# A transformer block on one core: the last addition moved to ScalarE and a DMA, another split of the convolution, and a new order

## The chip, the cores and the metric

The kernel runs on one core of a Trainium2 chip. A core has five engines that work side by side, each through its own list of instructions in order: TensorE (PE, matrix products; its weight loads are listed as PEld), VectorE (DVE), ScalarE (ACT), GpSimd (POOL) and SyncE (SP, which only issues transfers). Sixteen DMA engines move data; they are fed by the queues of SP, ACT and POOL. The metric is the device time of one execution in microseconds (us); less is better.

## The reference

The input x has 16 images of 128 channels and 96 x 96 pixels, all float32. One block is computed, image by image:

```
x_hwc = x.transpose(0, 2, 3, 1)
xn1 = _layernorm(x_hwc, ln1_w, ln1_b)
attn_out = _attention(xn1, wq, wk, wv, wp)     # 8 heads; channels attend to channels, over all pixels
x = x + attn_out.transpose(0, 3, 1, 2)
xn2 = _layernorm(x_hwc, ln2_w, ln2_b)          # x_hwc of the new x
h1 = einsum('bchw,oc->bohw', xn2, w_in)        # 128 -> 512 channels
h2 = depthwise 3x3 convolution of h1, padded by 1
h3 = gelu(h2, approximate=False)
x = x + einsum('bchw,oc->bohw', h3, w_out)     # 512 -> 128 channels
```

The attention needs one 128 x 128 matrix per image (the Gram matrix of the normalised pixels), so the whole image must have passed the first layer norm (LN1) before its attention is known. The second part needs only neighbouring rows.

## The kernel before, in words

**Tiling.** An image is cut in 8 bands of 12 rows (1152 pixels), a band in 3 units of 4 rows (384 pixels); 16 images make 128 bands. Channels lie on the 128 partitions. The 512 hidden channels are 4 chunks of 128.

**LN1 and LN2** take groups of four times 128 pixels: PE transposes them into PSUM (`forth`, L602), DVE takes statistics (`stats`, L609), POOL makes the variance and the power -0.5 of it (`variance` L616, `power` L620), for LN2 DVE makes a shift (`shift`, tile `nb_b`, L624), ACT scales into a buffer `zT` (L647, L651; for the start DVE takes half of it, L634, L638), PE adds to the Gram matrix (L661, LN1 only) and transposes back (L692), and ACT places the result in the padded image `xn` (L696, L698). While one image is in its second part, LN1 of the next runs beside it.

**x2.** PE applies the attention's matrix (L560). ACT writes the sum with a bias to the band buffer `xb` (`mixed`, L569), and a DMA issued by POOL adds x to it in flight (`add_x`, L572). There are 6 `xb` buffers. The first 6 bands of image 0 have x in `xb` already, and DVE adds (L566).

**Hidden part.** For a chunk of a band (`conv_job`), PE makes the hidden rows (L877), ACT copies them to SBUF (`kept`, L882; two rows from the band above by `halo`, L873). The depthwise convolution has 9 taps. One comes with the first DVE instruction; of the 8 others, two, or three for chunk 1, are products by ACT (`products`, L890, tiles `pr`, 5 buffers) that POOL-issued DMAs add to each other and to the result (L899); the rest are DVE instructions (`tap`, L895: one scalar_tensor_tensor over 128 x 1152 each). ACT applies gelu (L903). The very last job has no products.

**Chunk 3 on PE.** In some bands (`by_pe`) chunk 3 is not convolved so: 9 matmuls per unit with a composed 128 x 128 matrix per tap (`by_matmuls`, L945) make the convolved hidden rows in PSUM directly, and ACT applies gelu from there (L951). Before, these are every second band, and 6 of the last 8.

**Out.** Four matmuls per unit (`ffn_out`, L968) sum the chunks in PSUM, DVE adds that to `xb` (L975), SP stores the band (L979).

**Order.** Nothing runs in the order of the loops. Each operation is recorded with an estimated duration and a place, a number that its kind's entry in the table `AT` shifts; `Plan.order` then runs a list scheduling with those numbers, buffers included, and the instructions are emitted in the order of the planned starts. Operations with a smaller place go first when several are ready. At run time each engine follows its list and waits on semaphores, so an instruction that waits holds up all behind it on its engine. POOL's list holds both the small arithmetic of the layer norms and the issues of the accumulating DMAs.

Of the kernel before, what the change touches and what calls it, by code (L numbers as in the profile page):

```python
# [17 lines left out]
UR = 4  # L18
BR = 12
PE_CHUNK = 3  # L20
PE_BANDS = (0,)
PE_OF = 2
# [4 lines left out]
THIRD, THIRD_OF, THIRD_CHUNK = (0, 1, 2), 3, 1  # L27
# [3 lines left out]
X1_BUFS, XB_BUFS, PR_BUFS, H3_BUFS, ZT_BUFS = 2, 6, 5, 10, 3  # L31
IN_TURN = ("tr", "h3", "pr", "xb", "x1")
AT = dict(
    weights=86, zeros=34, load_a=-17.95, forth_a=-1.35, stats_a=-23.85, variance_a=50.15, power_a=-16.45,
    scaled_a=6.1, gram=-31.8, back_a=-145.85, place_a=68, attention=-19.55, mix=-17.6, residual=60.15,
    mixed=-98.2, add_x=-22.85, forth_b=-2, stats_b=-5.55, variance_b=52.05, power_b=-11, shift_b=-76.95,
    scaled_b=98.5, back_b=-23.15, place_b=20.55, halo=21.65, hidden=1.35, kept=-79.55, products=8.4,
    add_last=-64.4, tap=0.1, add_first=-14.5, gelu=-63.5, conv=1.15, conv_gelu=-1.85, out=4.9, add=-43.45,
    store=47.1,
# [6 lines left out]
T_WEIGHTS = 20000  # L46
# [160 lines left out]
def tile_restormer_block(  # L207
# [133 lines left out]
    grams, mats, h3s, staged = {}, {}, {}, {}  # L341
# [5 lines left out]
    def at(kind, place):  # L347
        return place + AT[kind]
# [56 lines left out]
    def weights(p):  # L405
# [17 lines left out]
        def transposed(parts, kept, gives):  # L423

            key = ("weights", next(names))
            h = ("h", key)
            d = {}

            def forth():
                d["pt"] = bank(key)  # L430
                for k, part in enumerate(parts()):
                    nc.tensor.transpose(d["pt"][:, k * P : (k + 1) * P], part, ident)

            pe(440, at("weights", p), forth, mine, [h])
            dve(700, at("weights", p), lambda: kept(d["pt"]), [h], [("w", g) for g in gives] + mine[1:])
# [56 lines left out]
        def unit_parts():  # L492
# [3 lines left out]
        op("ACT", 400, at("load_a", p), loads, [], mine, T_WEIGHTS, dma=2 * T_MOVE)  # L496
# [3 lines left out]
            lambda: [v["wqk"][:, :P], v["wqk"][:, P:], v["wp"], wv_sb], keep_qkp, ["qk"]  # L500
# [6 lines left out]
        dve(700, at("weights", p), unit_parts, [mine[0], ("w", "in")], [mine[1]])  # L507
        transposed(
            lambda: [v["wt"][:, n, :] for n in range(NCH)],
            lambda pt: nc.vector.tensor_scalar(winT.rearrange("p n c -> p (n c)"), pt, w2, None, ALU.mult), ["in"],  # L510
        )
        transposed(
            lambda: [v["wout"][:, n * P : (n + 1) * P] for n in range(NCH)],
            lambda pt: nc.vector.tensor_copy(woutT.rearrange("p n c -> p (n c)"), pt), ["out"],
        )
        for t0 in (0, 4, 8):
            ts = range(t0, min(t0 + 4, 9))
            dve(170 * len(ts), at("weights", p), lambda ts=ts: comp_parts(ts), [mine[0]], [mine[1]])
            transposed(
                lambda ts=ts: [v["wt"][:, t % 4, :] for t in ts],  # L520
# [23 lines left out]
    def norm(i, second, place_of):  # L544
# [8 lines left out]
        def x2(s, u):  # L553
# [22 lines left out]
            if loaded:  # L576
                pe(t_mm(UT), at("mix", s), mix, [*ins, xtok(u)], [pm])
                dve(t_dve(UT), at("residual", s), residual, [pm], [xtok(u)])
                return
            pe(t_mm(UT), at("mix", s), mix, ins, [pm, xtok(u)])  # L580
            act(t_act(UT, 1) - 43, at("mixed", s), mixed, [pm], [xtok(u)])
            if u % UPB == UPB - 1:
                xb = [xtok(b * UPB + k) for k in range(UPB)]
                add(at("add_x", s), add_x, [], xb)

        def pixels(s, m):
# [5 lines left out]
            by_dve = QT // 2 if early else 0  # L592

# [32 lines left out]
            def zT(q):  # L626
                zTs[q] = zT_bufs[plan.slot["zT", (name, q)]]
                return zTs[q]
# [38 lines left out]
            for q, tr in zip(qs, trs):  # L667
                units = {t // TPU: None for t in range(q * QT, (q + 1) * QT)}
                pe(110 * QT, at("forth" + ab, s), lambda q=q: forth(q), [xtok(u) for u in units], [tr])
            for j in range(QB * QT // 2):  # L670
                dve(341, at("stats" + ab, s), lambda j=j: stats(j), [trs[2 * j // QT]], [bt])
            op("POOL", T_VARIANCE, at("variance" + ab, s), variance, [], [bt], T_VARIANCE + 33 + SLACK)
            op("POOL", T_POWER, at("power" + ab, s), power, [], [bt], T_POWER + 33 + SLACK)
            if second:
                dve(80, at("shift" + ab, s), shift, [], [bt])
            for h, (q, tr) in enumerate(zip(qs, trs)):
                zt, sh = ("zT", (name, q)), s + STEP["scaled"] * h
                if by_dve:
                    dve(by_dve * 240, at("scaled" + ab, sh), lambda q=q: also_scaled(q), [tr, bt], [(*zt, 0)])
                act((QT - by_dve) * (343 if second else 250), at("scaled" + ab, sh), lambda q=q: scaled(q), [tr, bt], [(*zt, 1)])  # L680
                if not second:
                    pe(QT * 220, at("gram", sh), lambda q=q: gram(q), [(*zt, 0), (*zt, 1), ("w", "ones")], [("g", i)])

        def channels(s, u):
# [27 lines left out]
            pe(110 * TPU, at("back" + ab, s), back, [("zT", (name, q), k) for q in quads for k in range(2)], [pb])  # L712
            act(t_act(UT, 1) - 43 if second else t_copy(UT), at("place" + ab, s), place, [pb, ("w", "shift")], [z_unit(i, u)])
            for k, r, row, of in copies:
                act(225, at("place" + ab, s), lambda k=k, r=r, row=row: place_row(k, r, row), [pb, ("w", "shift")], [("z", k, of)])
# [243 lines left out]
    def ffn_out(p, g, s):  # L959
# [13 lines left out]
        def add():  # L973
            xt = x_unit(xbs, i, s + b * UPB)
            nc.vector.tensor_add(xt, d["po"], xt)  # L975

# [7 lines left out]
        dve(t_dve(UT), at("add", p), add, [po], [("xb", (i, b), s)])  # L984
        if g == NG - 1:
            move(at("store", p), lambda: store(s, 1), [("xb", (i, b), s)], [], T_MOVE / UPB)
        elif s == UPB - 1:
            move(at("store", p), lambda: store(0, UPB), [("xb", (i, b), k) for k in range(UPB)], [], T_MOVE)
# [64 lines left out]
```

## Time and profile before

| what | value |
|---|---|
| median of 3 executions | 4179.18 us (4177.25 to 4179.65) |
| the profiled execution | 4194.94 us, its span 4193.2 us |
| PE busy | 4151.7 us, 99% |
| DVE busy | 4073.2 us, 97% |
| ACT busy | 3682.0 us, 88% |
| POOL busy | 2593.8 us, 62% |
| DMA traffic | 827.63 MB, mean 197 GB/s; HBM 53 GB/s |
| mean granted TensorE clock | 0.998 |

The profile is of one execution, and its rows are compared with its own span; the execution with the profiler was 15.8 us longer than the median without. A group of instructions is given as: line, engine, operation, out<-in, count, then busy time, mean duration in ns, and idle time of the engine just before them with what ended it. A float32 matmul over 128 x 384 appears as two records. Busy time of PE is modelled at its ends, and the duration of a DVE or ACT instruction overlaps the start of the next, so the price of one more instruction is better read from the distance of starts in a row of equal instructions.

### The profile page before, as it was taken

What the parts mean: (1) busy time and instruction counts of PE and PEld (TensorE: products, weight loads), DVE (VectorE), ACT (ScalarE), POOL (GpSimd) and SP (SyncE); (2) the same over time, 40 slices, a digit from 0 to 9 for tenths busy, and PEclk for the clock granted to TensorE, in tenths of its full rate; (3) what the DMA queues carried; (4) which work ended last, traced back from release to release, by engine and by line L of the source; (5) the groups of instructions that cost most, each with busy time, mean ns of one, the idle gap of its engine ahead of it and who ended that gap; (6) DMA issues with size and microseconds to landing.
All of it is one profiled execution on the core that took longest, in us unless ns stands there. A gap on an engine that the chain in (4) does not pass through costs nothing. (4 is left out here: it accounts for less than half of the span.)

```text
span 4193.2 us, 52283 instructions
## 1 busy us (share of the span) xinstructions
PE 4151.7 (99%) x17457; PEld 2684.0 (64%) x17457; DVE 4073.2 (97%) x4676; ACT 3682.0 (88%) x6970; POOL 2593.8 (62%) x2373
## 2 busy tenths in 40 slices
PE   8999999999999999999999999999999999999999
PEld 6666666666666666666666666666666666666565
DVE  6999999999999999999999999999999999999998
ACT  4988989899899888999988899898998989889885
POOL 3656666566675666657666566656656667565542
PEclk9999999999999999999999999999999999999999
DMA  2999999999999999999999999999999999999997
GB/s 78 192 191 201 208 198 208 189 213 201 206 207 204 206 196 204 203 202 207 198 206 198 197 206 198 206 201 201 208 197 212 195 207 202 191 205 199 196 197 160
DMA packets 203934, 827.63 MB, mean 197 GB/s; under 512 B 23568, under 2 KB 24976, under 8 KB 203664
## 3 DMA queue, kind: packets, MB, share of 16 engines
q0 software_dynamic: 164160, 672.47, 82.9%
q1 hardware_dynamic: 37152, 151.01, 9.8%
q8 instruction: 138, 2.26, 0.2%
q10 hardware_dynamic: 2352, 0.81, 0.1%
q14 instruction: 132, 1.08, 0.1%
HBM read 148.26 MB, written 75.50 MB: 53 GB/s over the span
## 5 line engine op out<-in xcount | busy, mean ns | idle before, releaser
L895 DVE SCALAR_TENSOR_TENSOR h<-h,ratio,h 128x1152 f32<-128x1152 f32 x2104 | 2933.0, 1415 | 5.0
L890 ACT ACTIVATE pr<-h,ratio 128x1152 f32<-128x1152 f32 x1018 | 1304.2, 1290 | 21.8 <-DMA pr<-pr 20.3
L945 PE MATMUL h<-xn,comp 128*128 128x384 f32 x3564 | 1277.4, 486 | 1.7 <-ACT h L951 0.9
L968 PE MATMUL h<-h,woutT 128*128 128x384 f32 x3072 | 1112.8, 487 | 1.8 <-ACT h L903 0.7
L877 PE MATMUL h<-xn,winT 128*128 128x384 f32 (+1 forms) x2676 | 1048.4, 500 | 2.1 <-DVE x L975 1.1
L945 PEld LDWEIGHTS h<-xn,comp 128*128 128x128 f32 x3564 | 647.3, 189 | 394.4 <-issue 10.4
L899 POOL DMA_DIRECT2D pr<-pr x573 | 545.7, 960 | 475.1 <-ACT pr L890 325.7
L968 PEld LDWEIGHTS h<-h,woutT 128*128 128x128 f32 x3072 | 560.7, 190 | 345.1 <-issue 7.5
L882 ACT COPY h<-h 128x384 f32<-128x384 f32 (+1 forms) x1338 | 658.1, 521 | 139.7 <-PE h L877 122.4
L877 PEld LDWEIGHTS h<-xn,winT 128*128 128x128 f32 x2676 | 479.5, 190 | 290.9 <-issue 49.7
L899 POOL DMA_DIRECT2D h<-pr x445 | 433.9, 977 | 356.7 <-DVE h L895 93.7
L895 DVE SCALAR_TENSOR_TENSOR h<-h,ratio 128x1152 f32<-128x1152 f32 x446 | 630.1, 1419 | 11.5 <-ACT h L882 7.8
L903 ACT ACTIVATE h<-h 128x1152 f32<-128x1152 f32 x448 | 533.7, 1192 | 51.9 <-DMA h<-pr 48.0
L616 POOL TENSOR_SCALAR ve_b<-st_b 128x4 f32<-128x4 f32 x288 | 364.3, 1265 | 310.8 <-DVE st_b L609 304.6
L620 POOL TENSOR_TENSOR rstd_b<-ve_b,mhalf 128x4 f32<-128x4 f32 x288 | 525.1, 1823 | 13.9
L620 POOL TENSOR_TENSOR rstd_a<-ve_a,mhalf 128x4 f32<-128x4 f32 x288 | 498.2, 1730 | 15.7 <-POOL ve_a L616 0.2
L616 POOL TENSOR_SCALAR ve_a<-st_a 128x4 f32<-128x4 f32 x288 | 323.9, 1125 | 292.2 <-DVE st_a L609 291.7
L651 ACT ACTIVATE zT<-pT_b,nb_b,rstd_b 128x128 f32<-128x128 f32 x1132 | 431.4, 483 | 45.7 <-DVE nb_b L624 45.4
L647 ACT ACTIVATE zT<-pT_a,rstd_a 128x128 f32<-128x128 f32 x1080 | 314.7, 398 | 39.3 <-POOL rstd_a L620 38.4
L661 PEld LDWEIGHTS g<-zT 128*128 128x128 f32 x2304 | 294.4, 192 | 50.0 <-ACT zT L647 7.9
L661 PE MATMUL g<-zT 128*128 128x129 f32 x2304 | 307.1, 276 | 3.3 <-ACT zT L647 3.3
L560 PE MATMUL h<-xn,mwT 128*128 128x384 f32 x768 | 283.5, 490 | 1.2 <-ACT x L569 0.8
(172 smaller groups left out, 3605.4 us busy)
## 6 DMA issues: line engine op xcount, KB each, us to landing
pr<-pr POOLq DMA_DIRECT2D x573, 576.0 KB, 6.9
h<-pr POOLq DMA_DIRECT2D x445, 576.0 KB, 7.4
x<-in_x_dram SPq DMA_DIRECT2D x128, 576.0 KB, 6.5
out_dram<-x SPq DMA_DIRECT2D x127, 576.0 KB, 5.6
x<-in_x_dram POOLq DMA_DIRECT2D x122, 576.0 KB, 7.7
out_dram<-x SPq DMA_DIRECT2D x3, 192.0 KB, 1.9
weights<-in_L_conv_w_in_dram ACTq DMA_DIRECT2D x1, 256.0 KB, 10.7
weights<-in_L_conv_w_out_dram ACTq DMA_DIRECT2D x1, 256.0 KB, 11.6
```

The lines of the kernel that those rows point to most:

```text
L616: nc.gpsimd.tensor_scalar(ve, d["mv"][:, :, 2], 1.0 / C, EPS, ALU.mult, ALU.add)
L620: nc.gpsimd.tensor_tensor(rstd, d["ve"], mhalf, ALU.pow)
L651: nc.scalar.activation(zT(q)[:, k, :P], d["pT", q][:, k, :], AF.Identity, bias=d["nb"][:, t : t + 1], scale=d["rstd"][:, t : t + 1],)
L661: nc.tensor.matmul(grams[i][:, : P + 1], lhsT=zt[:, :P], rhs=zt, start=(q == 0 and k == 0), stop=(q == NU * TPU // QT - 1 and k == QT - 1),)
L877: nc.tensor.matmul(rows(ph), lhsT=winT[:, n, :], rhs=window(xn, r0 + r, e - r, 1), start=True, stop=True)
L882: nc.scalar.copy(window(h1_, r, e - r, 1), rows(d.pop(("ph", r))))
L890: nc.scalar.activation(to, shifted(t), AF.Copy, scale=ratio[:, n, t : t + 1])
L895: nc.vector.scalar_tensor_tensor(h3, shifted(t), ratio[:, n, t : t + 1], onto, ALU.mult, ALU.add)
L899: nc.gpsimd.dma_start(out=to, in_=d["pr", t], accum_op=ALU.add)
L903: nc.scalar.activation(h3, h3, AF.Gelu)
L945: nc.tensor.matmul(d["pc"], lhsT=comp[:, t, :], rhs=window(xn, r0 + dy, UR, dx), start=(t == 0), stop=(t == 8),)
L968: nc.tensor.matmul(rows(d["po"]), lhsT=woutT[:, n, :], rhs=h3s[g, n][:, s * UR : (s + 1) * UR, :], start=(k == 0), stop=(k == NCH - 1),)
```

## The change

Four things:

1. **Final addition.** For all bands but the last two, DVE no longer adds PSUM to `xb`. ACT copies each of the band's three units from PSUM into a buffer of the `pr` pool (`evicted`), and after the third one DMA issued by POOL adds the buffer to `xb` (`add_out`); then SP stores as before.
2. **No third product.** `THIRD` is empty, so chunk 1 has two products like the others, and one more tap on DVE.
3. **Chunk 3 on PE** in bands 0, 2, 4, ... 12 of every 15 (counted from the end) in place of every second; the last 8 bands as before.
4. **Start and order.** LN1 of image 0 scales into buffers of the `h3` pool, a pair of groups in each (9 of 10 buffers hold all 18 groups), in place of 3 `zT` buffers in turn. The weights are loaded by their own place, and the part of their preparation that only the hidden part needs has a place of its own (`late`). All entries of `AT` are new, and image 0 has entries of its own (`..._0`).

```diff
-PE_BANDS = (0,)
-PE_OF = 2
+PE_BANDS = (0, 2, 4, 6, 8, 10, 12)
+PE_OF = 15
-THIRD, THIRD_OF, THIRD_CHUNK = (0, 1, 2), 3, 1
+THIRD, THIRD_OF, THIRD_CHUNK = (), 3, 1
+ADD_OF, ADD_BY_DMA = 1, (0,)
-AT = dict(weights=86, zeros=34, ... stats_b=-5.55, variance_b=52.05, power_b=-11, shift_b=-76.95, ...)
+AT = dict(load_w=10.25, weights=-46.8, ... stats_b=-219.5, variance_b=53.7, power_b=-244.15, shift_b=-78.6, ...)
...
             def zT(q):
-                zTs[q] = zT_bufs[plan.slot["zT", (name, q)]]
+                if q in zTs:
+                    return zTs[q]
+                if not apart:
+                    zTs[q] = zT_bufs[plan.slot["zT", (name, q)]]
+                    return zTs[q]
+                two = [k for k in (q - q % 2, q - q % 2 + 1)]
+                t = h3p.tile([P, BR * W], F32, tag="h3", name=f"zT_{two[0]}")
+                for k in two:
+                    zTs[k] = t[:, k % 2 * QT * (P + 1) : (k % 2 + 1) * QT * (P + 1)].rearrange("p (t c) -> p t c", c=P + 1)
+                    nc.gpsimd.memset(zTs[k][:, :, P:], 1.0)
                 return zTs[q]
...
-        def add():
+        def add_here():
             xt = x_unit(xbs, i, s + b * UPB)
             nc.vector.tensor_add(xt, d["po"], xt)
+
+        def evicted():
+            if s == 0:
+                outs[g] = prp.tile([P, BR, W], F32, tag="pr", name=f"out_{g}")
+            nc.scalar.copy(outs[g][:, s * UR : (s + 1) * UR, :], rows(d["po"]))
+
+        def add_out():
+            nc.gpsimd.dma_start(out=xbs[i, b], in_=outs[g].rearrange("p r w -> p (r w)"), accum_op=ALU.add)
...
-        dve(t_dve(UT), at("add", p), add, [po], [("xb", (i, b), s)])
+        band_ = [("xb", (i, b), k) for k in range(UPB)]
+        if g < NG - 2 and g % ADD_OF in ADD_BY_DMA:
+            act(t_copy(UT), at("evicted", p), evicted, [po], [("pr", ("out", g), s)])
+            if s == UPB - 1:
+                add(at("add_out", p), add_out, [("pr", ("out", g), k) for k in range(UPB)], band_)
+        else:
+            dve(t_dve(UT), at("add", p), add_here, [po], [("xb", (i, b), s)])
```

## The prediction

> **What bounds the kernel now.** I read the busy times first, then the same by stage, then the chain of waits at the end, then what DVE waited for.
>
> ```profile
> PE 4151.7 (99%) x17457; PEld 2684.0 (64%) x17457; DVE 4073.2 (97%) x4676; ACT 3682.0 (88%) x6970; POOL 2593.8 (62%) x2373
> ```
>
> PE and DVE are both nearly full, so the question is how much true work each has. A stage table (busy time, number of instructions, granted clock, DMA share):
>
> ```profile
> core 0: us, PE busy (x) PEld busy (x) DVE busy (x) ACT busy (x) POOL busy (x), PEclk, DMA share, GB/s
> 0.00:104.00 104.00, 87.63 (x541) 71.28 (x542) 65.84 (x195) 49.42 (x129) 39.75 (x97) 0.95 0.25 77
> 104.00:4140.00 4036.00, 4014.39 (x16764) 2583.96 (x16763) 3966.23 (x4448) 3613.30 (x6815) 2547.22 (x2269) 1.00 0.95 201
> 4140.00:4193.00 53.00, 49.64 (x154) 28.77 (x152) 41.11 (x36) 19.33 (x28) 6.88 (x8) 1.00 0.63 147
> ```
>
> DVE idles 104 - 65.84 = 38.2 us in the start, 4036 - 3966.23 = 69.8 us in the long middle, and 53 - 41.11 = 11.9 us at the end: 119.8 us in all. That is all that any change can win on DVE without taking work from it.
>
> ```profile
> L895 DVE SCALAR_TENSOR_TENSOR h<-h,ratio,h 128x1152 f32<-128x1152 f32 x2104 | 2933.0, 1415 | 5.0
> ...
> L945 PE MATMUL h<-xn,comp 128*128 128x384 f32 x3564 | 1277.4, 486 | 1.7 <-ACT h L951 0.9
> L968 PE MATMUL h<-h,woutT 128*128 128x384 f32 x3072 | 1112.8, 487 | 1.8 <-ACT h L903 0.7
> ...
> L975 DVE TENSOR_TENSOR x<-h,x 128x384 f32<-128x384 f32 x384 | 214.2, 558 | 8.8 <-PE h L968 6.8
> ```
>
> ```profile
> 3920.34 5.81 PE h L945 x18
> 4174.16 15.49 PE h L968 x48
> ```
>
> The chain of waits of the last 500 us is matmul after matmul; its two lines give the pace of PE, 5.81/18 = 0.323 us per record of 384 columns. At that pace, with 0.404 for 480 columns and 0.11 for the small ones, PE's work is 1151 (L945) + 992 (L968) + 722 + 178 (L877) + 248 (L560) + 257 (L661) + 502 (4608 transposes) + some 50 = 4100 us of a 4193 us span. DVE's is 4073. So PE is the tighter, by 27 us, and neither has much room.
>
> **The change part by part.** Durations are of the profiled execution; its span stands 14.0 us above the median of 4179.18, and I carry differences over.
>
> *PE.* Bands with chunk 3 on PE: 3564/54 = 66 before; 56 + 6 = 62 after. Removed 4 x 54 records x 0.323 = 69.8 us; added, hidden rows of 4 chunks without halo, 4 x (4 x 0.404 + 2 x 0.323) = 9.0 us. PE: 4100 to 4039.
>
> *DVE.* Removed 378 of the 384 adds: successive starts (an add, then a tap) lie 0.467 us apart, 176.5 us. Added: taps go from 445 x 6 - 128 + 8 = 2550 to 449 x 6 + 8 = 2702; starts in a row of taps lie 1.328 us apart, so 152 x 1.328 = 201.9 us. DVE: +25.4, to 4098.6 us. So the two engines change places: work on the fuller engine falls by 1 us only, and what counts is how much of DVE's idle time goes once PE has 61 us of slack.
>
> *ACT.* 378 copies at 0.37 between starts (140 us) and 4 jobs' copies, products and gelus (18) come; 128 products at 1.157 (148) and 12 small gelus (5) go: +5 us, on an engine that idles 420 us in the middle. A copy waits for its matmuls as the add did on DVE (6.8 us in 16 waits); behind it on ACT stand the copies of hidden rows and the products, and behind those wait DVE's taps (7.8 us now) and POOL's issues; the PSUM bank (one of 4) is held as long. Taken as hidden, since ACT is the less full engine.
>
> *DMA.*
>
> ```profile
> q0 software_dynamic: 164160, 672.47, 82.9%
> q1 hardware_dynamic: 37152, 151.01, 9.8%
> ```
>
> The 1140 accumulating transfers take 0.829 x 4193 / 1140 = 3.05 us each of all sixteen engines. After: 449 + 449 + 126 + 122 = 1146. 6 more: 18 us, and six more issues of about 0.96 us on POOL. The engines are at 0.95 in the middle, so 5% (about 200 us) covers it; without cover it costs 18 us, and with longer queues could cost more. `add_out` stands in POOL's list behind the third copy on ACT, as `add_x` stands behind its copies; that wait costs POOL 79.4 us in 122 issues, so some 82 us, with variance and power queued behind it, for which the shift on DVE waits; the 128 third additions that go waited 325.7/573 = 0.57 us each, 73 us. No net change. SP's stores now wait for a landing, median 6.9 us, rather than for DVE; SP waits over 1100 us for adds anyway, and `xb` comes free some 8 us later in a cycle of 6 bands (196 us). Zero, bounded by 8 us once for each time the pool runs dry.
>
> *`pr` buffers.* A band's sum stays in one of 5 for two steps between units and a landing, about 20 us; the third product that goes held one for about 10. Taken as zero; bounded above by a stalled product per band, seen in rows as 20.3 us in all today.
>
> *Start.* Before the first hidden matmul at 92.0 us PE has 62.6 us of work, and starts at 5.6: 24 us are gaps or slow clock. In the built order of the changed kernel PE has 3 us more work before that point (LN1 of image 1 is further on), DVE 1 us more before its first tap. The weights move behind the first four groups on ACT's list: five issues of about 0.45 us there, with landings of about 12 us, 15 us before use; 18 more memsets of about 0.1 us stand in front on POOL, done before x lands at 5.6. LN1 of image 0 already keeps PE full at 1.66 us per group, so bigger buffers can only close the gaps around it: between no gain and 8 us; DVE's idle there 30 to 42, I take 32, nearest to closing one third of PE's gaps.
>
> *End.* DVE's 11.9 us are mostly waits for PE (3.4 for one tap, 3.3 for adds); with PE ahead I take 7, between 6 and 14.
>
> *Middle.* DVE's waits:
>
> ```profile
> DVE nb_b L624 <- POOL rstd_b L620: 38.3, 35, 2.0
> DVE x L975 <- PE h L968: 6.8, 16, 2.9
> DVE st_b L609 <- PE pT_b L602: 6.1, 15, 0.9
> DVE x L566 <- PE h L560: 5.9, 6, 2.4
> ```
>
> About 16 of the 69.8 us are waits that PE ended directly; with PE slack they go (0 to 16 remain). 15.6 us are short gaps and the attention chain; they stay. The rest, 38 us, is the wait of the shift for POOL's power, `w`. It does not come from PE:
>
> ```profile
> 1106.77 5.06 POOL L616 TENSOR_SCALAR ve_b<-st_b 128x4 f32<-128x4 f32 x1
> 1105.03 2.75 DVE L895 SCALAR_TENSOR_TENSOR h<-h,ratio 128x1152 f32<-128x1152 f32 x2
> 1107.69 4.08 DVE L895 SCALAR_TENSOR_TENSOR h<-h,ratio,h 128x1152 f32<-128x1152 f32 x3
> 1112.97 0.16 DVE L624 SCALAR_TENSOR_TENSOR nb_b<-st_b,rstd_b 128x4 f32<-128x4 f32 x1 [1.20 <-POOL rstd_b L620]
> ```
>
> A 0.2 us operation on POOL took 5.06 us, ending when a row of five taps on DVE ended, and the shift behind them waited 1.20. POOL gets in only between taps, and not each time. In the built order, one or more POOL instructions stand between variance and power in 142 of 288 groups (121 before; two or more in 4, before 28), and two or fewer taps between statistics and shift in 9 groups (20 before). By this trace's waits sorted by the first count (0.078 us without one, 0.243 with one), w would be 45; by the second 36; by the sum now 38. Below these: LN2's statistics and power move to the front of their queues (`stats_b`, `power_b`), so POOL gets the work sooner. I take 30, in 20 to 62; the top is 0.215 us for every group, near what a group with one issue between pays.
>
> [...]
>
> *Sum.* 4098.6 + 32 + 7 + (0 + 30 + 15.6) = 4183.2, 10.0 below 4193.2: 4169 us as the median.
>
> **Rivals.**
>
> *Nothing moves (same).* The change does not do what it says, since DVE stays as full as PE was: w keeps 38, the start 38.2. 4098.6 + 38.2 + 7 + 53.6 = 4197.4, so about 4183; with half of those gains 4176. For it: work on the fuller engine falls by 1 us. Against: PE's gaps in the start look closable.
>
> *POOL's power is late (slower).* Place: the shift in DVE's list, every LN2 group. Price w = 62: span 4215, median 4201. It decides from w = 48: then the span passes 4201.6, which is 0.2% above. For it: 152 more taps, 378 fewer adds. Against: two or fewer taps in front of the shift become rarer.
>
> *DMA engines become the pace (slower).* At 0.95 in the middle, 3909 us of work grow by 18 us; if time follows, 4193 x 18/3909 = 19.6 us: 4199. For it: the middle's share. Against: DVE names DMA in no wait of the middle.
>
> *A better start still and few waits (faster).* Start 30, end 6, w 20: 4098.6 + 30 + 6 + 35.6 = 4170: 4156. Slightly below, about 4148, lies what is left if half of the short gaps go as well.
>
> *TensorE slows when it has gaps.*
>
> ```profile
> 144.42 0.33 PE L692 MATMUL pB_b<-ident,zT 128*128 128x128 f32 x1 [2.18 <-ACT zT L651]
> 147.03 5.08 PE L968 MATMUL h<-h,woutT 128*128 128x384 f32 x8 [0.46 <-ACT h L882]
> ```
>
> After waits of 2.18 and 0.72 us and shorter ones, 8 records took 5.08 us in place of 2.6, with 0.72 of the clock granted from 141 to 153 us. In the middle it is 1.00. With 61 us of slack in short pieces such places may come there too; each costs PE 2.5 us, which the slack covers 24 times: no change of the sum.
>
> **How the numbers follow.** 0.2%, 8.4 us, is about what a measurement of this kernel can tell from no change. The forecast 0.34 and the better start 0.08: 0.42 faster. Nothing moves: 0.25. POOL late 0.21, DMA 0.08, `pr` or `xb` short 0.04: 0.33 slower. The likeliest alone spans 4160 to 4171. The range goes from 4148 to 4206, POOL's case included, with about 0.05 left out below and 0.13 above.
>
> **What the profile after would show.** Right: 2702 taps and 6 adds on DVE; PE busy clearly below 99% in the middle while DVE stays above 98%; waits of DVE for PE under 6 us in the middle; the wait for POOL's power at or below 35 us; DVE idle under 45 us in the middle and 33 in the start. Wrong: w over 48 us; a chain of waits with DMA in it; DVE waiting for ACT's copies; a first tap later than 97.3 us.

## The result and the profile after

The changed kernel takes 4195.46 us (median of 7 executions, 4187.10 to 4201.36), the kernel before 4179.65 us on the same chip (7 executions, 4177.06 to 4182.02). The ratio is 1.0038, 95% interval 1.0026 to 1.0049: slower by 15.8 us. Forecast were 4169 us and a gain.

Busy times of the changed kernel (part 1 of the page), and its three stages:

```profile
PE 4120.2 (98%) x17265; PEld 2648.1 (63%) x17265; DVE 4089.8 (97%) x4450; ACT 3697.8 (88%) x7232; POOL 2606.6 (62%) x2397
```

```profile
core 0: us, PE busy (x) PEld busy (x) DVE busy (x) ACT busy (x) POOL busy (x), PEclk, DMA share, GB/s
0.00:104.00 104.00, 88.67 (x570) 72.80 (x571) 69.42 (x198) 52.56 (x136) 43.99 (x120) 0.98 0.29 90
104.00:4140.00 4036.00, 3977.34 (x16530) 2543.90 (x16529) 3974.60 (x4216) 3621.13 (x7061) 2553.57 (x2267) 1.00 0.95 201
4140.00:4198.00 58.00, 54.19 (x168) 31.43 (x167) 45.76 (x38) 24.13 (x36) 9.08 (x11) 1.00 0.67 153
```

The first line gives, for PE, its weight loads, DVE, ACT and POOL, the busy time, its share of the span and the number of instructions. The span is 4197.8 us. DVE idles 104 - 69.42 = 34.6 us in the start, 4036 - 3974.60 = 61.4 us in the middle and some 12 us at the end: 108.0 us. PE idles 58.7 us in the middle.

The profile of before that the forecast was built on was of a long execution: 4194.94 us, where the others lay between 4177 and 4182. A second profile of the same kernel (experiment `before_again`, below) has a span of 4180.7 us, and this is the one to hold the changed kernel against:

```profile
PE 4146.4 (99%) x17457; PEld 2684.4 (64%) x17457; DVE 4072.1 (97%) x4676; ACT 3687.8 (88%) x6970; POOL 2570.7 (61%) x2373
```

```profile
0.00:104.00 104.00, 87.84 (x542) 71.35 (x543) 66.08 (x195) 49.77 (x130) 40.00 (x98) 0.95 0.24 78
104.00:4140.00 4036.00, 4021.44 (x16803) 2591.59 (x16802) 3975.26 (x4454) 3624.18 (x6823) 2525.59 (x2270) 1.00 0.95 202
```

DVE's idle time is 4180.7 - 4072.1 = 108.6 us there: 37.9 in the start, 60.7 in the middle, 10 at the end. It is 108.0 after the change. PE's idle time in the middle is 14.6 us there. So by the records nothing was won on DVE's idle time, and DVE's busy time grew by 17.7 us: that is the 17.1 us between the two spans.

The records overlap a little (a tap's record lasts 1403 ns on average after the change, the next instruction's start follows 1329 ns behind its own, by the median), so a short wait can hide in busy time. A stricter account uses distances of starts: the work of an engine is the sum, over its instructions, of the 25th percentile of the distance to the next start for that kind of instruction, and the rest of the span is idle. All accounts of work below are made so, each from one profiled execution.

| kernel | span | PE work / idle | DVE work / idle |
|---|---|---|---|
| before, second profile | 4180.7 | 4089.1 / 91.6 | 4035.7 / 145.0 |
| changed | 4197.8 | 4030.8 / 167.0 | 4062.4 / 135.4 |

DVE: +26.7 us of work, -9.6 us of idle time, together +17.1. PE: -58.3 us of work, and 75 us more idle time. The slack that the change gave PE stayed on PE.

What DVE waited for, first after the change, then in the second profile of before (engine, waiting tile and line, what ended the wait; us in all, times, longest):

```profile
DVE nb_b L632 <- POOL rstd_b L628: 30.1, 26, 3.3
DVE st_a L617 <- PE pT_a L610: 14.6, 13, 3.4
...
DVE st_b L617 <- PE pT_b L610: 6.3, 9, 2.3
DVE st_a L617 <- PE h L610: 5.4, 4, 2.2
DVE h L918 <- PE h L991: 5.3, 1, 5.3
```

```profile
DVE nb_b L624 <- POOL rstd_b L620: 26.7, 26, 2.0
...
DVE x L975 <- PE h L968: 7.2, 17, 2.9
...
DVE st_b L609 <- PE pT_b L602: 6.2, 14, 1.9
DVE st_a L609 <- PE pT_a L602: 5.3, 11, 1.8
```

The waits in front of the final adds went with the adds. The waits for the transposes, 11.5 us, became 20.9 (in the middle alone 9.8 became 15.4). The rows of the middle that PE ended sum to 15.9 us before (6.2, 4.0, 3.6, 1.7 and 0.4) and to 18.8 after (9.1, 6.3 and 3.4), though PE now has 167 us to spare. PE's own idle time in the middle, sorted by what ended it, names ACT for 13.9 of 14.6 us before and for 55.6 of 58.7 us after. One place shows how PE's spare time and DVE's waits go together. This is the chain of waits of the changed kernel around 660 us (start, duration, what):

```profile
651.21 11.15 DMA h<-pr
662.36 0.02 issue
662.38 0.03 ACT pr L913
662.41 1.13 issue
663.55 0.46 ACT h L905
664.01 1.06 ACT h L926
665.07 0.38 ACT xn L721
665.45 0.04 issue
665.49 0.55 PE pB_a L715 x3
666.04 1.24 PE h L567 x2
667.28 1.28 PE h L968 x2
668.56 1.11 PE h L991 x2
669.67 0.33 PE pB_a L715 x3
670.00 0.44 PE pT_a L610 x4
```

and the same place on PE, ACT and DVE (in brackets the idle time before it, and what ended it):

```profile
662.38 1.26 ACT L913 ACTIVATE pr<-h,ratio 128x1152 f32<-128x1152 f32 x1 [2.86 <-DMA h<-pr]
665.49 0.55 PE L715 MATMUL pB_a<-ident,zT 128*128 128x128 f32 x3 [1.91 <-ACT xn L721]
670.47 0.43 DVE L617 BATCH_NORM_STATS2 st_a<-pT_a 128x6 f32<-128x256 f32 x1 [3.45 <-PE pT_a L610]
```

ACT waits 2.86 us until a transfer has emptied a `pr` buffer. Three ACT instructions later comes the copy that frees the PSUM bank that PE's next transposition back needs: PE waits 1.91 us. Behind that, pairs of records of 384 columns take 1.24, 1.28 and 1.11 us in place of 0.65, with a granted clock of 0.50 from 665.95 to 669.37 us (last section), and the transposes that DVE's statistics need are in line behind them: DVE waits 3.45 us. At this place PE was not short of time; it was held by ACT, and ACT by a transfer. PE's gaps of over 1 us in the middle are 16 (29 us in all) after the change and 2 (3.6 us) before.

### The profile page after: what moved, and what is told of

The parts are those of the page before. It is cut to its first block, busy times and chain, and to the rows that moved or that the text cites. A ratio compares the mean times of both kernels' runs of the same rounds, so it can differ in the third digit from the quotient of the medians.

```text
span 4197.8 us, 52159 instructions
## 1 busy us (share of the span) xinstructions
PE 4120.2 (98%) x17265; PEld 2648.1 (63%) x17265; DVE 4089.8 (97%) x4450; ACT 3697.8 (88%) x7232; POOL 2606.6 (62%) x2397
## 4 chain that ended last, share of the span: by engine, by line
PE 59%; DVE 27%; ACT 5%; POOL 4%; DMA 2%; issue 2%; ACTq 0%; POOLq 0%; DVEq 0%
DVE h L918 24%; PE h L968 16%; PE h L991 15%; PE h L900 12%; PE g L678 4%; PE h L567 4%; PE pB_a L715 2%; PE pT_b L610 2%; PE pB_b L715 2%; PE pT_a L610 2%; DVE st_a L617 1%; DMA h<-pr 1%; DVE st_b L617 1%; ACT pr L913 1%; POOL rstd_b L628 1%
## 5 line engine op out<-in xcount | busy, mean ns | idle before, releaser
L918 DVE SCALAR_TENSOR_TENSOR h<-h,ratio,h 128x1152 f32<-128x1152 f32 x2252 | 3105.2, 1403 | 4.1
L913 ACT ACTIVATE pr<-h,ratio 128x1152 f32<-128x1152 f32 x898 | 1159.8, 1296 | 44.0 <-DMA h<-pr 29.8
L968 PE MATMUL h<-xn,comp 128*128 128x384 f32 x3348 | 1195.2, 486 | 2.5 <-ACT h L905 2.5
L991 PE MATMUL h<-h,woutT 128*128 128x384 f32 x3072 | 1138.7, 488 | 5.8 <-ACT h L926 2.8
L900 PE MATMUL h<-xn,winT 128*128 128x384 f32 (+1 forms) x2700 | 1073.2, 502 | 6.1 <-ACT h L905 3.4
L968 PEld LDWEIGHTS h<-xn,comp 128*128 128x128 f32 x3348 | 609.1, 190 | 369.0 <-issue 8.1
L991 PEld LDWEIGHTS h<-h,woutT 128*128 128x128 f32 x3072 | 559.6, 190 | 351.8 <-issue 11.6
L922 POOL DMA_DIRECT2D pr<-pr x449 | 441.9, 984 | 406.2 <-ACT pr L913 368.9
L628 POOL TENSOR_TENSOR rstd_a<-ve_a,mhalf 128x4 f32<-128x4 f32 x288 | 539.7, 1875 | 12.7
L624 POOL TENSOR_SCALAR ve_a<-st_a 128x4 f32<-128x4 f32 x288 | 340.9, 1184 | 260.9 <-DVE st_a L617 254.0
L624 POOL TENSOR_SCALAR ve_b<-st_b 128x4 f32<-128x4 f32 x288 | 325.8, 1131 | 194.5 <-DVE st_b L617 188.8
L567 PE MATMUL h<-xn,mwT 128*128 128x384 f32 x768 | 294.1, 496 | 11.7 <-ACT h L905 6.6
```

What stands on the lines that cost most here:

```text
L567: nc.tensor.matmul(rows(pm), lhsT=mats[i][0], rhs=interior(i, u), start=True, stop=True)
L624: nc.gpsimd.tensor_scalar(ve, d["mv"][:, :, 2], 1.0 / C, EPS, ALU.mult, ALU.add)
L628: nc.gpsimd.tensor_tensor(rstd, d["ve"], mhalf, ALU.pow)
L900: nc.tensor.matmul(rows(ph), lhsT=winT[:, n, :], rhs=window(xn, r0 + r, e - r, 1), start=True, stop=True)
L913: nc.scalar.activation(to, shifted(t), AF.Copy, scale=ratio[:, n, t : t + 1])
L918: nc.vector.scalar_tensor_tensor(h3, shifted(t), ratio[:, n, t : t + 1], onto, ALU.mult, ALU.add)
```

## The experiments

Three theories were to be told apart. Theory A: DVE sets the pace of the changed kernel, so 25 us more of its work is 25 us more time, whatever PE has to spare. Theory B: the engines hold each other up through waits in a fixed order, none sets the pace alone, and the new order may be what costs. Theory C: the DMA engines set the pace. Differences below are each against the kernel before on the same chip: so many us over or under it, with the ratio's 95% interval.

### The order fixed, some 50 us of one engine's work taken away

The instructions and their order stay; only their lengths change, so a part of the result is not computed.

```diff
 after_dve:
-nc.vector.scalar_tensor_tensor(h3, shifted(t), ratio[...], onto, ALU.mult, ALU.add)
+c = W if t == left[0] else W - 2
+nc.vector.scalar_tensor_tensor(h3[:, :, :c], shifted(t)[:, :, :c], ratio[...], onto[:, :, :c], ALU.mult, ALU.add)
 after_pe:
+c = W if k == 0 else W - 7
-rows(d["po"]), lhsT=woutT[:, n, :], rhs=h3s[g, n][:, s * UR : (s + 1) * UR, :],
+rows(d["po"])[:, :, :c], lhsT=woutT[:, n, :], rhs=h3s[g, n][:, s * UR : (s + 1) * UR, :c],
 after_act:
-h3 = h3_of(g, n)[:, s0 * UR : s1 * UR, :]
+h3 = h3_of(g, n)[:, s0 * UR : s1 * UR, : W - 12]
 after_dma:
-nc.gpsimd.dma_start(out=to, in_=d["pr", t], accum_op=ALU.add)
+flat = [v.rearrange("p r w -> p (r w)")[:, : BR * W - 24] for v in (to, d["pr", t])]
+nc.gpsimd.dma_start(out=flat[0], in_=flat[1], accum_op=ALU.add)
```

> The changed kernel in its own order, with each of the 2252 accumulating taps that are not the first of their job leaving out the last 2 of 96 columns (so a part of the convolution is not computed). Taken from DVE: 2252 x 24 elements x about 1.04 ns (1152 elements in 1.2 us of a 1.328 us start distance) = 56 us. Theory A, DVE sets the pace of the changed kernel: the time falls by 45 us or more, to about 4145. Theory B, the engines hold each other up through waits in a fixed order and none sets the pace alone: 15 to 35 us, PE taking over with its 4039 us of work and its gaps. Theory C, the DMA engines set it (0.95 in the middle): under 10 us.

> The changed kernel in its own order, with the out product's matmuls of the second to fourth chunk leaving out the last 7 of 96 columns (so a part of the sum is not computed). Taken from PE: 2304 records x 28 columns x 0.84 ns = 54 us, on top of the 61 us that the change took. Theory A: PE has slack already, and the 9.1 + 6.3 us that DVE waits for PE's transposes in the middle are the most that can go: 0 to 10 us. Theory B: 15 to 35 us. Theory C: none.

> The changed kernel in its own order, with the gelu after the taps leaving out the last 12 of 96 columns (a part of the gelu is not computed). Taken from ACT: about 450 x 144 elements x 0.83 ns = 54 us. Theory A: DVE waits for ACT hardly anywhere, 0 to 5 us. Theory B: PE's gaps in the middle end by ACT (scaled groups, gelu) and DVE's wait for PE's transposes behind them: 8 to 25 us. Theory C: none.

> The changed kernel in its own order, with the products' accumulating transfers moving 1128 of 1152 elements per partition (a part of the convolution is not computed). Taken from the sixteen DMA engines: 898 x 3.05 us x 24/1152 = 57 us of 3909 in the middle. Theory A and B: under 6 us. Theory C: 40 us or more, to about 4150.

| run | us | ratio to before (95%) | over before | gain on the changed kernel's +15.8 |
|---|---|---|---|---|
| after_dve | 4169.77 | 0.9980 (0.9970 to 0.9989) | -9.1 | 24.9 |
| after_pe | 4183.19 | 1.0011 (1.0002 to 1.0021) | +4.3 | 11.5 |
| after_act | 4187.78 | 1.0023 (1.0012 to 1.0035) | +8.9 | 6.9 |
| after_dma | 4193.06 | 1.0036 (1.0023 to 1.0049) | +14.2 | 1.6 |

DVE's shorter taps took 51.7 us of its work (4062.4 to 4010.7), half of which came off the time; PE's 57.5 us gave 11.5 and ACT's 54 (3528.8 to 3474.9) gave 6.9, both between what A and B expected; ACT's gain is no larger than the intervals. Theory A alone falls, since it asked for 45 us; so does theory C: 57 us less of the DMA engines' work is 1.6 us, within the interval nothing. DVE is the tightest engine of the changed kernel and not the only one. Where did the other 27 us of DVE go? Mostly into waits for PE: DVE's idle time in the records grew by 18.8 us, and 15.7 of these are waits that PE ended.

```profile
DVE nb_b L632 <- POOL rstd_b L628: 29.3, 29, 2.5
DVE st_a L617 <- PE pT_a L610: 15.6, 27, 3.1
DVE st_b L617 <- PE pT_b L610: 11.9, 27, 2.0
DVE h L919 <- PE h L994: 9.1, 3, 6.9
```

Those lines are of `after_dve`: PE's transposes hold DVE 54 times where they did 22 times. In `after_pe` the rows of the middle that PE ended fall from 18.8 to 8.7 us: so some of these waits do go when PE has less to do, and some do not.

### Before, a second profile and the same two cuts

The edits are those of `after_dve` and `after_pe`, made in the kernel before; `before_again` has none.

> The kernel before once more, unchanged, for a second profile. The sum of the prediction took 14 us from the profiled span (4193.2) to the median (4179.2), while the changed kernel's profiled span lies only 2.3 us above its median. If the first profile of before was simply a long execution, the span here is 4176 to 4186, with DVE idle near 106 instead of 119.8 us; if the profile itself lengthens this kernel, the span is again 4190 or more.

> The kernel before in its own order, with the accumulating taps that are not the first of their job leaving out the last 2 of 96 columns (part of the convolution is not computed), as was done to the changed kernel, where it took 47 us of busy time from DVE and 26 us from the time. Here DVE should lose about 44 us. Theory A (before, PE sets the pace): 0 to 8 us. Theory B (the engines hold each other up, none sets the pace alone): 15 to 30 us.

> The kernel before in its own order, with the out product's matmuls of the second to fourth chunk leaving out the last 7 of 96 columns (part of the sum is not computed). Taken from PE: 54 us of work, the same as in the changed kernel, where the time fell by 12 us. Theory A: DVE becomes the bound after the first 27 us, so 25 to 40 us. Theory B: 10 to 25 us. If this is near 0, the 61 us of PE's work that the change took were worth nothing in the first place.

`before_again`: 4182.09 us with a span of 4180.7, so the first profile was a long execution, not a long profile. Its busy times are those of the first within 2 us on DVE; 11 of the 12.5 us between the two spans are DVE's idle time, and 11.6 us are in one row, the shift's wait for POOL's power: 38.3 us in the first, 26.7 in the second.

`before_dve`: 4175.38 us, ratio 0.9980 (0.9971 to 0.9989), a gain of 7.6 us for 48 us of DVE's work. `before_pe`: 4168.70 us, 0.9967 (0.9957 to 0.9977), 14.3 us for 55 us of PE's. The first is what theory A expected, the second what theory B did. In the kernel before, PE is the tighter engine by this measure, as the forecast had it, though the two intervals overlap a little; but 55 us less on it are worth 14, not 27 or more. A cut on one engine runs into the other.

`before_pe` is also the cleanest test of what slack on PE does to DVE's waits, because nothing else changes, not even the order. The waits for the transposes stay, in the middle 9.8 us before and 11.0 here:

```profile
DVE st_b L609 <- PE pT_b L602: 6.9, 7, 3.2
DVE st_a L609 <- PE pT_a L602: 4.1, 5, 1.4
```

The waits in front of the adds fall from 4.0 to 0.9, and all rows of the middle that PE ended from 15.9 to 12.6 us.

### Both cuts at once in the changed kernel

> The changed kernel with both shortenings at once: taps without their last 2 columns and out matmuls without their last 7 (part of the convolution and of the sum is not computed). Alone they took 26 and 12 us off the time. If DVE's and PE's work hold each other up, so that what one gives the other takes back, both together give more than the 38 us of the sum, 45 to 55; if the rest is ACT, POOL and DMA, 30 to 40.

4153.58 us, ratio 0.9936 (0.9921 to 0.9951): 40.7 us off the changed kernel's +15.8, where the two alone gave 24.9 + 11.5 = 36.4. That lies between the two expectations, and the 4 us over the sum of the two are within the intervals: a coupling of PE and DVE alone is not shown. 109 us of work less on the two gave 41; what holds the rest was not tested.

### The split of work and the order, one at a time

```diff
 p1_order_only (in the changed kernel), p2_bands (the first hunk alone)
-PE_BANDS = (0, 2, 4, 6, 8, 10, 12)
-PE_OF = 15
+PE_BANDS = (0,)
+PE_OF = 2
-THIRD, THIRD_OF, THIRD_CHUNK = (), 3, 1
+THIRD, THIRD_OF, THIRD_CHUNK = (0, 1, 2), 3, 1
-ADD_OF, ADD_BY_DMA = 1, (0,)
+ADD_OF, ADD_BY_DMA = 1, ()
 b62_work_only (in the kernel before)
-PE_BANDS = (0,)
-PE_OF = 2
+PE_BANDS = (0, 2, 4, 6, 8, 10, 12)
+PE_OF = 15
 b64_work_only (in the kernel before): PE_BANDS = tuple(range(0, 28, 2)); PE_OF = 29
```

> The changed kernel's order table, loads and buffers for the first image, with the old split of work: the add on DVE, the third product in chunk 1, chunk 3 on PE in every second band. Work per engine as before (PE 4100, DVE 4073, DMA engines 18 us less than after). If the split is what costs, the time is at or under before, 4165 to 4182, by the shorter start (34.6 in place of 38.2 us of DVE idle). If the new order costs, it is at or above the changed kernel, 4190 to 4215. Such a table is fitted to one split, so up to 10 us more would not tell against the first.

> The changed kernel in its own order table with chunk 3 on PE in every second band again (66 bands, not 62): PE +61, DVE -32 us. By the prices found on the changed kernel (DVE 26 us for 52, PE 12 for 54) -16 + 14 = -2: 4194. If PE becomes the bound again at 4100 us of work, 4200 to 4215. If DVE alone sets the time, 4165 to 4180.

> The kernel before with its own order table, adds, third products and buffers; only chunk 3 goes to PE in 62 bands as in the changed kernel, not 66. PE's work falls by 61 us, exactly as in the change; DVE's rises by 4 jobs x 6 taps (5 in a third of chunk 1's case, not concerned) x 1.33 = 32 us, against 25 in the change. By the prices that the shortened runs gave on the kernel before (14.3 us for 54 us of PE, 7.6 for 48 us of DVE): -16 + 5 = -11, to about 4171. By the price of DVE in the changed kernel (26 us for 52): -16 + 16 = 0, 4182. If moving work from PE to DVE is itself what made the change slower, it is 4190 or more.

> As the run with 62 bands, with 64: PE -30, DVE +16 us. By the same two prices -6 or 0: 4176 to 4182.

| run | table | add, third product | bands on PE | us | ratio (95%) | over before | PE work / idle | DVE work / idle |
|---|---|---|---|---|---|---|---|---|
| p1_order_only | new | old | 66 | 4196.18 | 1.0032 (1.0020 to 1.0043) | +13.2 | 4089.1 / 104.6 | 4036.2 / 157.5 |
| p2_bands | new | new | 66 | 4185.67 | 1.0019 (1.0010 to 1.0028) | +7.2 | 4089.5 / 92.6 | 4031.1 / 151.0 |
| changed | new | new | 62 | 4195.46 | 1.0038 (1.0026 to 1.0049) | +15.8 | 4030.8 / 167.0 | 4062.4 / 135.4 |
| b62_work_only | old | old | 62 | 4206.38 | 1.0068 (1.0053 to 1.0083) | +27.4 | 4028.5 / 178.0 | 4067.6 / 138.9 |
| b64_work_only | old | old | 64 | 4230.20 | 1.0127 (1.0112 to 1.0142) | +51.2 | 4058.8 / 167.1 | 4051.9 / 174.0 |

The trade of bands, 61 us off PE for 32 us on DVE, was made twice. Under the old table it costs 27.4 us; under the new one 8.6 (from `p2_bands` to the changed kernel, two intervals that only just touch). `p2_bands` lies between its expectations and meets none of the three. The account is of the same form both times: DVE's work +31.9 and +31.3, its idle time -6.1 and -15.6. The idle time on PE grew by 86 and 74 us. So 61 us taken from PE bought 6 to 16 us on DVE, and DVE's work was paid in full. The waits of the middle that PE ended did not go either: 15.9 us before and 23.7 in `b62_work_only`, 18.2 in `p2_bands` and 18.8 in the changed kernel. But a new split also makes the planner fit a new order, and these pairs of runs do not separate the two. The stage table of `b62_work_only` shows the same picture as the changed kernel, with nothing of the final addition, the start or the table changed:

```profile
104.00:4140.00 4036.00, 3969.24 (x16530) 2549.49 (x16529) 3979.58 (x4460) 3610.98 (x6812) 2501.65 (x2271) 0.99 0.95 202
```

The exchange of final adds for third products (`p1_order_only` to `p2_bands`) is worth about 6 us, of the size of the intervals, for 5 us less of DVE's work. The new table with the new start costs: with the old split, and so the old work on every engine, DVE idles 12.5 us more than before and the time is 13.2 us up. `b64_work_only` fits none of its expectations: it moves half as much work as `b62_work_only` and costs nearly twice as much, and both engines idle some 170 us. So what a split costs under a table made for another one is not a price of the work moved.

### Parts of the order

`table_only` has the old split, start and buffers, and only the general entries of the new table. `start_only` has the old split, table and buffers, and only the new places of `load_w`, `weights`, `late` and `zeros`; `start_ln1` adds the larger buffers. `after_old_ln1_buffers` is the changed kernel with this edit:

```diff
-apart = i == 0 and not second
+apart = False
...
-return ("h3", ("zT", q // 2), q % 2) if i == 0 and not second else ("zT", (name, q))
+return ("zT", (name, q))
```

> The old split, the old loads' places and the first image's LN1 in its old buffers and with the old entries for it; only the general entries of the order table are the changed kernel's. The old split with the whole new order and the new buffers took 13 us more than before. If the table costs that, 4190 to 4205 here; if the start and the first image's buffers cost it, 4178 to 4186.

> The changed kernel with the first image's LN1 back in three buffers in turn, all else as it is. The prediction gave the start 6 us less of DVE's idle time for closing gaps around LN1, of which the profiles show 3.6 (38.2 to 34.6). If the larger buffers bring that, 4198 to 4203 here; if they bring nothing, 4193 to 4198; if they hold up the first jobs, whose tiles share these buffers, under 4193.

> The kernel before with its own split, table and LN1 buffers; only the places of the weights' loads, of their early and late preparation and of the zeros are the changed kernel's. DVE was 3.3 us further in the first 104 us with these. If that carries to the end, 4175 to 4178; if the list behind takes it back, 4179 to 4190.

> As start_only, with the first image's LN1 in the larger buffers too. In the changed kernel these buffers were worth nothing (1 us, within the measurement): the same time as start_only within 4 us. If they close PE's gaps around LN1 as the prediction took them to, 3 to 6 us under start_only.

| run | us | ratio (95%) | over before |
|---|---|---|---|
| table_only | 4189.46 | 1.0029 (1.0016 to 1.0042) | +10.4 |
| after_old_ln1_buffers | 4194.07 | 1.0040 (1.0025 to 1.0055) | +15.1 |
| start_only | 4200.03 | 1.0051 (1.0034 to 1.0067) | +21.6 |
| start_ln1 | 4199.34 | 1.0049 (1.0034 to 1.0064) | +20.9 |

The larger buffers are worth nothing, in two orders. The table alone loses most of what `p1_order_only` does, and the start alone loses more than both together: the parts do not add up. `start_only` is the one to remember: it changes four places in the first 100 us, no work, and costs 21.6 us, more than either of its expectations allowed. Its DVE idles 166.5 us against 145.0, and not in the start: the planner's choices behind it fall differently all the way, and its first tap is 1 us later than before, its 400th 8 us, its 2000th 19 us.

### Moving DVE's work to ACT and the DMA engines

```diff
 in p2_bands: p2_third6 (p2_third3 with 3 for 6)
-THIRD, THIRD_OF, THIRD_CHUNK = (), 3, 1
+THIRD, THIRD_OF, THIRD_CHUNK = (0,), 6, 1
```

> p2_bands with a third product by ACT and DMA in chunk 1 of every sixth band: 21 taps less on DVE (-28 us), 21 products of 1.157 more on ACT (+24), 21 accumulating transfers of 3.05 us more (+64 us of the sixteen DMA engines). By the prices of the changed kernel (DVE 0.5, ACT 0.17, DMA 0.04 us per us) -14 + 4 + 2 = -8 against p2_bands: 4178. If the DMA engines set the pace, +30 or more: 4215. If refitting of the order decides, anywhere between 4175 and 4205 without relation to the work.

> As p2_third6 in every third band: DVE -57, ACT +50, DMA engines +131 us. By the same prices -28 + 8 + 5 = -15 against p2_bands: 4171. If the DMA engines set the pace, 4230 or more.

`p2_third6`: 4205.75 us, ratio 1.0062 (1.0047 to 1.0077), 16.6 us over `p2_bands`; `p2_third3`: 4259.35 us, 1.0196 (1.0174 to 1.0218), 70 us over it, with 54 us less work on DVE (3977.0). The prices from the cut runs failed here, in sign. 16.6 us is within what a refitted order does; 70 us is more than any refit here did. Part 3 of the page, first of `p2_third3`, then of the changed kernel (packets, MB, share of sixteen engines' span):

```profile
q0 software_dynamic: 170064, 696.66, 84.5%
q1 hardware_dynamic: 37152, 151.01, 9.5%
```

```profile
q0 software_dynamic: 165024, 676.01, 83.3%
q1 hardware_dynamic: 37152, 151.01, 9.8%
```

0.845 x 4257 - 0.833 x 4198 = 100 us more in q0 than in the changed kernel, in a share that hardly rises. With that the DMA engines are the likely cause, but DVE's row that grew most names ACT's copies of hidden rows (47.5 us, 4.8 in the changed kernel), and that the engines are full at 0.95 was not shown directly. No version that computes the whole block is faster than the kernel before.

## Why the prediction was wrong, by its own steps

**The work on the engines: right.** 2702 taps and 6 adds, as counted. By distances of starts PE was to lose 61 us and lost 58.3; DVE was to gain 25.4 us and gained 26.7; ACT was to gain 5 and gained 4.6 (3524.2 to 3528.8). The 1146 accumulating transfers are hidden, as said (`after_dma`: 1.6 us for 57). DVE's own waits for ACT in the middle went from 7.3 to 5.0 us; but ACT is not hidden from PE, which waited for it 41.7 us longer in the middle.

**The sum, term by term.** The forecast's terms and what the records show: DVE's work 4098.6 and 4089.8, start 32 and 34.6, end 7 and 12.0, middle 45.6 and 61.4. The work term is 8.8 us too large because it adds 25.4 us of distances to 4073.2 us of busy time, which grew by less. That hid a part of the 23.4 us by which the idle terms were too small. The same mixture made PE the tighter engine by 27 us (4100 and 4073); by distances alone it was 53 (4089.1 and 4035.7), and the work on the fuller engine falls by 27 us, not by 1. So more was to be won on paper than the forecast took, and none of it came.

**The failed step: "what counts is how much of DVE's idle time goes once PE has 61 us of slack", and its working in *Middle*, "with PE slack they go".** It took the waits that PE ended, about 16 us, as a measure of PE being short of time, and let them go to 0. They are 18.8 us. The other two terms of the middle came out near the forecast, the wait for POOL's power with 30.1 for 30 and the rest with 12.5 for 15.6, so this one term is the whole miss of the middle. Slack on PE does not bring it to 0 in any pair of runs: 12.6 us stay in `before_pe` with the order fixed, 23.7 in `b62_work_only`, and 8.7 in `after_pe`, where PE has 58 us less work still. One reason is shown at 665 us: PE ends a wait also when it was itself held by ACT or a transfer, or runs slowly behind a gap (PE's 1.91 us behind ACT, ACT's 2.86 us behind a transfer, then 3.42 us at a clock of 0.50). How much of the 18.8 us is of that kind was not measured.

**The term that the sum lacked: the new order.** The forecast looked at the new places only for POOL's power and for the start. `p1_order_only` moves no work, has the new order and costs 13.2 us; `table_only` and `start_only` cost 10.4 and 21.6. The forecast has no term of this kind. Why one order of equal work is slower than another stays open.

**The `pr` buffers: a size that was wrong.** They were taken as zero, bounded by the 20.3 us that products waited. First before (second profile), then the changed kernel; the last number pair of a line is ACT's idle time in front of that group and what a DMA ended of it:

```profile
L890 ACT ACTIVATE pr<-h,ratio 128x1152 f32<-128x1152 f32 x1018 | 1304.8, 1290 | 19.8 <-DMA pr<-pr 18.8
L903 ACT ACTIVATE h<-h 128x1152 f32<-128x1152 f32 x448 | 533.7, 1192 | 39.5 <-DMA h<-pr 35.2
```

```profile
L913 ACT ACTIVATE pr<-h,ratio 128x1152 f32<-128x1152 f32 x898 | 1159.8, 1296 | 44.0 <-DMA h<-pr 29.8
L926 ACT ACTIVATE h<-h 128x1152 f32<-128x1152 f32 x452 | 545.3, 1209 | 13.8 <-DMA h<-pr 10.5
```

The products wait twice as long, the gelus a third as long; all of ACT's waits of the middle that a DMA ended are 50.1 us for 46.2. The chain at 660 us starts with such a wait for a `pr` buffer. `p1_order_only`, in which no sum is held in these buffers, has 36.5 us in front of the products in the middle, against 42.4 in the changed kernel and 18.9 before: most of the rise came with the order. What one more `pr` buffer would give was not tried.

**The base: a second error, of nearly the same size.** Of the 26.3 us between 4169.2 and 4195.5, the sum of the profile accounts for 4197.8 - 4183.2 = 14.6. The other 11.7 come from "its span stands 14.0 us above the median ... and I carry differences over": the profiled execution of before was a long one, that of the changed kernel stands 2.3 us above its median. The surplus sat in `w`, so it was also counted as something to win: `w` was forecast to fall from 38 to 30 and is 30.1, but it is 26.7 in the second profile of before. A sum made against an execution some 15 us longer than its fellows can keep the surplus or drop it; it can't both win it back and subtract it.

**The rivals.** *Nothing moves* has the mechanism that happened, DVE as full as PE was with its idle time in the records unchanged. That its span of 4197.4 us met the measured 4197.8 is luck: its work term is 8.8 us over and its start 3.6, its end is 5.0 under and its middle 7.8; the 14 us taken off then made it 4183. *POOL's power* is not the cause: w is 30.1, as forecast. Nor is `w` a price: with the old LN1 buffers it is 15.3 us, half, at the same time (4194.07 us for 4195.46), and in `after_dve_pe`, the fastest kernel here, 35.2. 30.1 and 15.3 us with the same 2702 taps, and 26.7 and 13.2 (`table_only`) with the same 2550, say that the order changes it by half; what the number of taps adds these runs do not separate. *DMA engines become the pace* falls for this change by `after_dma`; with some 100 us more DMA work (`p2_third3`) it may be true, which was not shown. *TensorE slows when it has gaps* was set at no cost because PE's slack covers it: at 665 us it did cost, since DVE waited behind it (3.45 us, of which about 1.6 by the estimate in the last section). Half clock after 160 us sums to 27.3 us in the changed kernel and to none in `before_again`; what all of it cost in time was not measured.

**The signs.** Of those named for a right forecast, 2702 taps and 6 adds, PE at 98.5% in the middle with DVE at 98.5%, and w at 30.1 us came; waits for PE under 6 us (18.8), DVE idle under 45 us in the middle (61.4) and under 33 in the start (34.6) did not. Of those named for a wrong one, a chain of waits with a DMA in it came, around 660 us; w over 48 us and a later first tap (94.9 us for 97.3) did not.

**What the change was worth by parts.** The table with the start +13 us, the exchange of adds for third products about -6, the bands +9: by differences of runs, with intervals of some 4 to 5 us each. A table is fitted to one split, so the +13 may be less of a property of the new table than of the mismatch, and so may the +27 of the bands under the old table; the whole new split under the old table was not tried. That the bands cost 9 us under the table fitted to them, against a split which that table was not fitted to, speaks for the trade itself being bad here. What in a list makes 10 to 50 us of difference at equal work stays open.

## What to carry to other kernels

In this kernel, with two engines both within a few per cent of the span, work did not trade between them at a fixed price: taking some 50 us away gave 8 to 25, moving 61 us off PE for 32 us on DVE cost 9 or 27 us by the order around it, and most of the slack on PE stayed idle, in waits that ACT ended. Take "DVE waits for PE" as PE being short of time only after looking at what PE itself waited for. Before building a sum on one profiled execution, hold its time against the other executions, and where an order is planned, measure first what a harmless change of the order costs (21 us here): terms smaller than that could not be forecast here from work alone.

## What the runs showed of the hardware that was not expected

A single gap of 1.91 us on PE was followed by half clock. The windows of the changed kernel, 1 us each, with the granted clock as the third number from the end:

```profile
665.00:666.00 1.00, 0.51 (x4) 0.51 (x5) 1.00 (x2) 1.00 (x5) 0.92 (x2) 0.98 1.08 217
666.00:667.00 1.00, 1.00 (x3) 0.47 (x2) 1.00 (x1) 1.00 (x4) 1.00 (x1) 0.50 1.07 212
667.00:668.00 1.00, 1.00 (x3) 0.61 (x2) 0.03 (x1) 0.68 (x2) 0.92 (x1) 0.50 1.06 212
668.00:669.00 1.00, 1.00 (x2) 0.39 (x2) 0.00 (x0) 0.40 (x1) 0.00 (x0) 0.50 1.03 207
669.00:670.00 1.00, 1.00 (x7) 0.72 (x6) 0.00 (x0) 0.09 (x1) 0.00 (x0) 0.82 0.41 78
```

From 665.95 to 669.37 us by the clock's own record it is 0.50. PE had been busy for 8.58 of the 8.60 us from 655 to 663.6 us, at a granted clock of 1.00.

The length of the gap alone does not explain it. In `after_act`, at the same place and in the same order, PE waits longer, and the clock stays at 1.00 from 660 to 670 us:

```profile
663.43 0.55 PE L715 MATMUL pB_a<-ident,zT 128*128 128x128 f32 x3 [2.34 <-ACT xn L721]
666.72 0.43 DVE L617 BATCH_NORM_STATS2 st_a<-pT_a 128x6 f32<-128x256 f32 x1 [2.28 <-PE pT_a L610]
```

DVE's wait is 2.28 us there and 3.45 in the changed kernel, though PE's gap is 0.43 us longer: by the author's estimate about 1.6 us of the 3.45 (3.45 - 2.28 + 0.43) are the price of the half clock. All slow stretches of the twenty traces but the last of each last 3.41, 6.83 or 10.24 us. In the changed kernel their starts lie whole multiples of 3.413 us apart: 22, 176, 240, 525, 818, 950 and 995 of them behind the first, at 65.2 us. Counted in these steps, the gap of 1.91 us lies in one (56% of it), that of 2.34 us in two (41 and 28%). After 160 us, all 38 full-clock steps of the twenty traces in which PE idled 58% or more were followed by half clock, and 15 of the 56 with 42 to 58%; of these the changed kernel has 2 of 2 (61 and 86%) and 4 of 7 (43 to 56%). Why the half clock follows in the one place and not in the other was not shown.

Half clock after 160 us sums to 27.3 us in the changed kernel and 37.5 in `b62_work_only`, to 13.7 in `start_only`, 3.4 in `p1_order_only` and none in `before_again` and `p2_bands`. It goes with PE's gaps of over 1 us, 29, 35, 14, 9, 4 and 8 us in the middle of these kernels.
